# Up products of the adapters in two rounds of eight banks per group, a quarter of them added by VectorE

## The chip, the cores and the metric

The kernel runs on one core of a Trainium2 chip. The metric is the device time of one execution in microseconds. Three runs of the kernel before gave 406.56, 407.0 and 408.68 us, median 407.0 us. A separate profiled execution took 406.23 us; from its first to its last instruction it spans 404.5 us, so 1.7 us lie around the span.

## What is computed

Two layers over eight batches of 256 tokens with 1024 features, all in 32-bit floats. The first adds to `x` a linear layer whose weight carries a per-batch sign matrix. The second adds a linear layer with low-rank adapters, one pair (A, B) chosen per batch out of 32:

```python
def _L1_cond_ref(x, adapter_mapping, W, b, lora_As, lora_Bs):
    base_out = jnp.einsum('bti,oi->bto', x, W) + b
    A = lora_As[adapter_mapping]
    Bm = lora_Bs[adapter_mapping]
    lora_h = jnp.einsum('bti,bir->btr', x, A)
    lora_out = jnp.einsum('btr,bro->bto', lora_h, Bm)
    return base_out + lora_out * SCALING
x = x + _L0_cond_ref(x, L0_cond_W, L0_cond_b, condB_coeff, mask_Bx4096x4096_ik1)
x = x + _L1_cond_ref(x, itok_B_0_23, L1_cond_W, L1_cond_b, L1_cond_lora_As, L1_cond_lora_Bs)
```

The residual `x` is folded into the weights as an identity. The "down" product is `x A` (1024 to 16), the "up" product is `h B` (16 to 1024); a seventeenth row carries the bias `b`.

## The kernel before

**Layers and groups.** Two groups of four batches. In each group the first layer builds the batches' weights and multiplies (lines 269 to 532), then the second layer (`second_layer`, L702) works on the four batches at once. The second layer of the first group runs from about 114 to 208 us, that of the second from about 308 us to the end.

**The second layer.** The product of the 1024x1024 weight with 1024 features by 4 x 256 tokens is done with seven outer products instead of eight (a fast matrix multiplication), each of which is again seven inner products of 256x256 blocks with 256 tokens. `plan` (L885) lists the outer ones; I call each a pass: A11, A12, S1, S2, S4, S3, A22, numbered 0 to 6. A pass is one call of `run` (L796). It needs three accumulators in PSUM, tiles of one bank each: X (begun by `begin`, L777, at the end of the pass before), Z and Y. The seven inner products go into X, Z or Y in a fixed order; each is four matrix products, eight matmul instructions on the chip (`product`, L719). An accumulator is used again without being cleared: what is read between two products is a partial sum. So a read of X must be over before the next product into X starts.

**Reads.** `read` (L781) takes a bank to SBUF: with no other operand ScalarE copies it (L783), with one VectorE adds it (L785). Pass 0 starts sums afresh (`seed` is None: first reads are ScalarE copies); pass 4 adds onto `c12`, so all seven reads are VectorE's. VectorE also forms the sums of the right-hand blocks for later passes (`outer_sum` L889 with 128x1024 subtractions at L897; `Right.sums` L687 with four 128x512 subtractions, L693 to L699), the final additions of quarters (`add`, L882, line L883 in the profile) and, during the first group, parts of the next group's weights (`next_weights`, L907, which end in an addition at L251). These are handed to `run` as the generator `beside`, and a `next(beside, None)` stands at chosen places between the products. `ordered` (L914) puts each step behind the last VectorE read issued so far.

**PSUM.** One pool of eight banks (L85) serves all of it. A new tile takes a bank that has come free; its first matmul waits until that bank's last reader is done.

**Adapters.** In pass 0 `down` (L757) computes `h` for the four batches. `up(i, u, dest)` (L736) computes one 256-row quarter of the adapter output for all four batches: four banks G, 8 matrix products (16 matmul instructions) with 32 contraction rows each, the four batches sitting on four different groups of 32 rows. Then ScalarE copies the four banks (L755) to `c11` and `c12` (or `c21` and `c22`). It is called four times per group: in pass 0 and pass 4 as `mid` (after the product a12 into Y) and as `late` (after the product a22 into X). So a pass with adapters has the order

```
a11>X  s1>Z  s2>X  a12>Y  [round 1: 4 G]  s3>X  (a11 of next >X')  a22>X  [round 2: 4 G]  s4>Z
```

**What the copies wait for.** After pass 0, VectorE adds `e1` (the result of pass 0) to the four quarters of `c11` (L939 to L945); pass 1 accumulates on `c11`. During pass 5, `add_e5` (L973) adds `e5` (the result of pass 2) to `c22`.

**Order.** The framework schedules instructions by its own estimates. `behind(what)` (L146) nails an instruction behind an earlier one on its engine: `product(first=True)` and `up` are held behind the last inner product and the last adapter product, so TensorE's order around the adapters is fixed by the text; VectorE's order is partly free.

**Blocks of the weight.** `load_leaves` (L711) issues the seven block loads of the next pass on SyncE's queue, in the order in which the pass uses them, with the next group's mask loads between a12 and s3 (`next_masks`).

Of the kernel before, what the change touches and what calls it, by code (L numbers as in the profile page):

```python
# [14 lines left out]
P = 128  # L15
OH = 512
CG = 2
OQ = 256
# [6 lines left out]
def kernel(  # L25
# [38 lines left out]
    nc = tc.nc  # L64
    B, NG, _, _, T = xT.shape
# [5 lines left out]
    GB = 4  # L71
    NGROUP = B // GB
    S = 32
# [21 lines left out]
    h_sb = const.tile([P, T], F32, tag="h", name="h_sb")  # L95
# [22 lines left out]
    lb_pad = const.tile([P, D], F32, tag="lb", name="lb_pad")  # L118
# [20 lines left out]
    anchors = {}  # L139
# [6 lines left out]
    def behind(what: str):  # L146
        return tc.issue_after(anchors[what].ins) if what in anchors else nullcontext()
# [118 lines left out]
    def bank(name):  # L266
        return psum.tile([P, 2, T], F32, tag="ps", name=name)
# [434 lines left out]
    def second_layer(group: int, y, first, first_steps, second):  # L702
# [6 lines left out]
        left_leaf, right = {}, {}  # L709

        def load_leaves(name):  # L711
            for n in ("a11", "s1", "s2", "a12", "s3", "a22", "s4"):
                if n == "s3":
                    next_masks(max(0, plan.index(name) - 1))
                t = lpool.tile([P, CG, OQ], F32, tag="l", name=f"l{group}_{name}_{n}")
                anchors["leaves"] = nc.sync.dma_start(t, leaf_at[name, n])
                left_leaf[name, n] = t

        def product(ps, l, r, first=False):  # L719
            order = [(c, j) for c in range(CG) for j in range(2)]  # L720


            with ExitStack() as place:
                for what in ("products", "inner", "adapters") if first else ("adapters",):
                    place.enter_context(behind(what))
                for c, j in order:
                    anchors["inner"] = nc.tensor.matmul(  # L727
                        ps[:, j, :],
                        lhsT=l[:, c, j * P : (j + 1) * P],
                        rhs=r[:, c, :],  # L730
                        start=first and c == 0 and j == 0,
                        stop=False,
                        skip_group_check=True,
                    )

        def up(i, u, dest):  # L736


            ps = [bank(f"G{b}_{group}_{i}{u}") for b in range(GB)]
            with behind("inner"):  # L740
                for j in range(2):
                    o = (2 * i + u) * OQ + j * P
                    for b in range(GB):
                        rows = slice(b * S, (b + 1) * S)
                        up = nc.tensor.matmul(  # L745
                            ps[b][:, j, :],
                            lhsT=lb_pad[rows, o : o + P],
                            rhs=h_sb[rows, :],
                            start=j == 0,
                            stop=j == 1,  # L750
                            skip_group_check=True,
                        )
            anchors["adapters"] = up
            for b in range(GB):
                nc.scalar.copy(dest[b // 2][u, b % 2], ps[b])  # L755

        def down():  # L757
            ph = bank(f"psh_{group}")
# [18 lines left out]
        def begin(n, name, r):  # L777
            banks[n] = bank(f"X_{group}_{n}")
            product(banks[n], left_leaf[name, "a11"], r.b[0, 0], first=True)

        def read(out, ps, other=None):  # L781
            if other is None:
                anchors["copies"] = nc.scalar.copy(out, ps)  # L783
                return anchors["copies"]
            own["reads"] = anchors["reads"] = nc.vector.tensor_add(out, ps, other)  # L785
            return anchors["reads"]
# [6 lines left out]

        UV = [(0, 0), (0, 1), (1, 1), (1, 0)]

        def run(n, name, r, seed, out, dest=None, beside=None, early=None, mid=None, late=None, then=None):  # L796

            leaf = {k: left_leaf.pop((name, k)) for k in ("a11", "s1", "s2", "a12", "s3", "a22", "s4")}  # L800
            other = seed or {uv: None for uv in UV}
            beside = beside or iter(())
            X = banks.pop(n)

            def done(uv):
                if dest:
                    store(out[uv], *dest, *uv)
                if then:
                    then(uv)

            read(out[0, 0], X, other[0, 0])
            Z = bank(f"Z_{group}_{n}")
            product(Z, leaf["s1"], r.t["t1"], first=True)
            if early:
                early()
            product(X, leaf["s2"], r.t["t2"])
            next(beside, None)
            read(out[0, 1], X, other[0, 1])
            Y = bank(f"Y_{group}_{n}")
            product(Y, leaf["a12"], r.b[1, 0], first=True)  # L820
            read(out[0, 0], Y, out[0, 0])
            done((0, 0))
            if mid:
                mid()
            if n + 1 == len(plan):
                finish(X, Z, leaf, r, other, out, dest, beside, done)
                return
            product(X, leaf["s3"], r.t["t3"])
            next(beside, None)
            read(out[1, 1], X, other[1, 1])  # L830
            read(out[1, 1], Z, out[1, 1])
            done((1, 1))
            load_leaves(plan[n + 1])
            begin(n + 1, plan[n + 1], right[plan[n + 1]])
            next(beside, None)
            product(X, leaf["a22"], r.t["t4"])
            read(out[1, 0], X, other[1, 0])
            done((1, 0))
            next(beside, None)
            if late:  # L840
                late()
            product(Z, leaf["s4"], r.b[1, 1])
            read(out[0, 1], Z, out[0, 1])
            done((0, 1))
            for _ in beside:
                pass
# [31 lines left out]
        def quads(name):  # L878
            two = [pair(f"{name}{u}_{group}") for u in range(2)]
            return {(u, v): two[u][:, v] for u, v in UV}  # L880

        def add(o, x):  # L882
            nc.vector.tensor_add(o, o, x)  # L883

        plan = ["A11", "A12", "S1", "S2", "S4", "S3", "A22"]  # L885
        right.update({"A11": first, "A12": second, "S4": Right(f"b22_{group}", b22)})
        big_t = {}

        def outer_sum(n, x, y, name):  # L889


            big_t[n] = [
                tpool.tile([P, TPH, T], F32, tag="T", name=f"T{n}_{group}_{v}") for v in range(2)
            ]
            right[name] = Right(f"T{n}_{group}", big_t[n])
            for v in range(2):
                nc.vector.tensor_sub(big_t[n][v], x[v], y[v])  # L897
                yield
            yield from right[name].sums()
# [7 lines left out]
        def next_weights(n):  # L907
            if group + 1 < NGROUP:
                while sevens[group + 1].made < n:
                    sevens[group + 1].begin(sevens[group + 1].made + 1)  # L910
                    yield


        def ordered(steps):  # L914

            while True:
                with behind("reads" if "reads" in own else "layer"):
                    if next(steps, True):
                        return
                yield  # L920
# [10 lines left out]
        for _ in chain(islice(s3, 1), ordered(second.sums()), islice(t1, 2)):  # L931
            pass
        e1, c11, c12 = quads("e1"), quads("c11"), quads("c12")
        lower = (c11, c12)
        run(
            0, "A11", first, None, e1,
            beside=chain((None, None), islice(s3, 4)),
            early=down,
            mid=lambda: up(0, 0, lower),  # L939
            late=lambda: up(0, 1, lower),  # L940
            then=lambda uv: add(c11[0, 0], e1[0, 0]) if uv == (1, 1) else None,
        )
        for uv in UV[1:]:
            with behind("reads"):
                add(c11[uv], e1[uv])  # L945
        t2 = ordered(outer_sum(2, b22, big_t[1], "S2"))
        run(
            1, "A12", second, c11, c11,
            dest=(0, 0),
            beside=chain(t1, s3, islice(t2, 2)),  # L950
        )
        e5 = quads("e5")
        run(
# [6 lines left out]
            beside=ordered(outer_sum(3, b22, b12, "S3")),  # L960
            then=lambda uv: add(c12[uv], e1[uv]),
        )
        c21, c22 = quads("c21"), quads("c22")
        upper = (c21, c22)
        run(
            4, "S4", right["S4"], c12, c12,
            dest=(0, 1),
            beside=chain(next_weights(2), ordered(outer_sum(4, b21, big_t[2], "A22"))),
            mid=lambda: up(1, 0, upper),
            late=lambda: up(1, 1, upper),  # L970
        )

        def add_e5():  # L973

            for uv in UV:
                with behind("reads"):
                    add(c22[uv], e5[uv])
                yield

        run(5, "S3", right["S3"], e1, e1, beside=chain(add_e5(), next_weights(4)), then=lambda uv: add(c21[uv], e1[uv]))  # L980


        next_masks(6)
# [168 lines left out]
```

## Time and profile before

| what | value |
|---|---|
| median of three runs | 407.0 us (406.56 to 408.68) |
| profiled execution, its own time | 406.23 us |
| its span, first to last instruction | 404.5 us |
| TensorE busy (matmuls) | 400.5 us, 99% |
| VectorE busy | 314.4 us, 78% |
| ScalarE busy | 137.1 us, 34% |
| granted TensorE clock | 1.00 throughout |
| up products: matmul instructions, ScalarE copies | 128, 32 |
| up rounds in the first group start at | 125.06, 131.52, 175.96, 182.41 us |
| up rounds in the second group start at | 318.80, 325.26, 369.70, 376.15 us |

The span is one execution seen by the hardware profiler. "Chain" means the chain of work that ended last, followed back from the last instruction; a timeline row gives start, duration, engine, line, output and inputs, and how often. G is the tile of an up product, X, Y, Z those of the inner products, `c` and `e` the quarters of results, T and T_t the right-hand sums.

### The profile page before, as it was taken

To read this page: it belongs to the slowest core of one execution; us is meant where nothing else is said; L and a number is where in the kernel's file an instruction comes from. 1 tells how busy PE (TensorE), PEld (TensorE's weight loads), DVE (VectorE), ACT (ScalarE), POOL (GpSimd) and SP (SyncE) were. 2 spreads that over 40 slices of the span, in tenths; PEclk is the share of its full clock that TensorE was granted. 3 is DMA by queue.
4 is the path that set the end of the run, shared out by engine and by line. 5 is a ranking of instruction groups with operands and counts; after the bars stand their busy time and mean duration, and the time that the engine had idled before them with its cause. 6 is when DMAs were issued, how large, how long until landed. Compare 5 with 4: busy or idle time off the path is not lost.

```text
span 404.5 us, 6810 instructions
## 1 busy us (share of the span) xinstructions
PE 400.5 (99%) x2562; PEld 359.9 (89%) x2562; DVE 314.4 (78%) x451; ACT 137.1 (34%) x223; POOL 52.5 (13%) x103
## 2 busy tenths in 40 slices
PE   8999999999999999999999999999999999999997
PEld 6888888899978888888899999999998788888886
DVE  2447695989983789987999999999926247898595
ACT  4444525773114213132131927528221420102200
POOL 0000152105944121011040000400000000000000
PEclk9999999999999999999999999999999999999999
DMA  8999999990799799676898858632022248555754
GB/s 291 398 402 396 400 412 417 412 354 4 244 366 345 239 340 318 233 233 214 301 382 333 331 157 278 237 110 54 28 80 73 78 131 236 167 156 158 212 170 158
DMA packets 41700, 99.56 MB, mean 246 GB/s; under 512 B 5700, under 2 KB 6340, under 8 KB 41668
## 3 DMA queue, kind: packets, MB, share of 16 engines
q1 hardware_dynamic: 32978, 76.11, 55.0%
q0 software_dynamic: 6240, 18.90, 12.5%
q10 hardware_dynamic: 2450, 4.13, 2.8%
q8 instruction: 20, 0.33, 0.3%
q14 instruction: 12, 0.10, 0.1%
HBM read 79.19 MB, written 19.92 MB: 245 GB/s over the span
## 4 chain that ended last, share of the span: by engine, by line
PE 98%; DMA 1%; DVE 0%; SPq 0%; issue 0%; DVEq 0%
PE X L727 23%; PE X L427 18%; PE ps L284 14%; PE Z L727 12%; PE Z L427 9%; PE ps L309 7%; PE Y L727 6%; PE Y L427 4%; PE G L745 2%; PE psh L762 2%; PE W L868 1%; DMA w_sb<-w0T 1%; DVE w L251 0%; SPq L203 0%; DVE c L785 0%
## 5 line engine op out<-in xcount | busy, mean ns | idle before, releaser
L243 ACT ACTIVATE w<-w,neg_c,two_c 128x1024 f32<-128x1024 int32 (+2 forms) x69 | 79.1, 1183 | 60.3 <-DMA w<-mask 55.8
L251 DVE TENSOR_TENSOR w<-w,w_sb 128x1024 f32<-128x1024 f32 (+2 forms) x69 | 77.9, 1146 | 26.7 <-ACT w L243 20.7
L284 PE MATMUL ps<-x,w 128*128 128x256 f32 x256 | 55.4, 380 | 0.0
L284 PEld LDWEIGHTS ps<-x,w 128*128 128x128 f32 x256 | 48.7, 190 | 6.5
L446 ACT ACTIVATE y<-X,b_sb 128x128 f32<-128x128 f32 x60 | 17.2, 368 | 69.9 <-PE X L427 69.9
L427 PE MATMUL X<-t,s 128*128 128x128 f32 x288 | 33.9, 276 | 0.0
L883 DVE TENSOR_TENSOR c<-c,e 128x512 f32<-128x512 f32 x48 | 32.0, 685 | 1.8 <-ACT c L755 1.8
L427 PEld LDWEIGHTS X<-t,s 128*128 128x128 f32 x288 | 33.0, 192 | 0.1
L755 ACT COPY c<-G 128x512 f32<-128x512 f32 x32 | 16.4, 600 | 39.0 <-PE G L745 39.0
L309 PE MATMUL ps<-x,w 128*128 128x256 f32 x128 | 28.9, 389 | 0.1
L309 PEld LDWEIGHTS ps<-x,w 128*128 128x128 f32 x128 | 24.9, 196 | 3.9 <-DVE w L251 0.5
L783 ACT COPY e<-X 128x512 f32<-128x512 f32 x16 | 9.4, 587 | 48.6 <-PE X L727 48.6
L785 DVE TENSOR_TENSOR c<-X,c 128x512 f32<-128x512 f32 x24 | 16.3, 688 | 8.8 <-PE X L727 8.7
L727 PE MATMUL X<-T_t,l_S_s 128*128 128x256 f32 x96 | 22.7, 379 | 0.0
L427 PE MATMUL X<-t,w 128*128 128x128 f32 x192 | 22.4, 275 | 0.0
L427 PEld LDWEIGHTS X<-t,w 128*128 128x128 f32 x192 | 21.9, 192 | 0.0
L363 DVE TENSOR_TENSOR s<-w,w 128x1024 f32<-128x1024 f32 x18 | 21.7, 1222 | 0.1
L727 PEld LDWEIGHTS X<-T_t,l_S_s 128*128 128x128 f32 x96 | 18.3, 190 | 2.4
L785 DVE TENSOR_TENSOR e<-Y,e 128x512 f32<-128x512 f32 x8 | 5.5, 691 | 17.6 <-PE Y L727 17.6
L427 PE MATMUL Z<-t,s 128*128 128x128 f32 x160 | 18.9, 275 | 0.0
L427 PE MATMUL X<-x,w 128*128 128x128 f32 x160 | 18.8, 275 | 0.0
L427 PE MATMUL Y<-x,w 128*128 128x128 f32 x160 | 18.7, 276 | 0.0
(145 smaller groups left out, 673.1 us busy)
## 6 DMA issues: line engine op xcount, KB each, us to landing
w<-mask SPq DMA_DIRECT2D x60, 512.0 KB, 7.2
l_S_s<-leaf_S_s SPq DMA_DIRECT2D x32, 256.0 KB, 2.7
x<-xT SPq DMA_DIRECT2D x31, 256.0 KB, 6.6
l_A_s<-leaf_A_s SPq DMA_DIRECT2D x24, 256.0 KB, 3.1
l_S_a<-leaf_S_a SPq DMA_DIRECT2D x24, 256.0 KB, 3.2
w<-w1T SPq DMA_DIRECT2D x16, 256.0 KB, 7.2
outT<-c POOLq DMA_DIRECT2D x15, 256.0 KB, 4.8
outT<-c ACTq DMA_DIRECT2D x15, 256.0 KB, 2.3
```

Source lines behind the costliest of these rows:

```text
L243: nc.scalar.activation(w[:, i, o], m[:, i, o], AF.Identity, bias=neg_c[:, b : b + 1], scale=two_c[:, b : b + 1],)
L251: weff_at[k] = nc.vector.tensor_add(w[:, i, o], w[:, i, o], w0_of(k)[:, i, o])
L284: nc.tensor.matmul(ps[j // 2][:, j % 2, :], lhsT=w[:, c, j * P : (j + 1) * P], rhs=x_sb[b, g][:, c, :],  start=first and j % 2 == 0, stop= ...
L309: nc.tensor.matmul(ps[ot // 2][:, ot % 2, :], lhsT=w[:, h, j * P : (j + 1) * P], rhs=x_sb[0, c // CG][:, c % CG, :], start=c == 0 and ot % ...
L363: anchors["weights"] = anchors["sums"] = op(s, self.w[x, a], self.w[y, a])
L427: anchors["products"] = nc.tensor.matmul(ps[:, j, :], lhsT=w[:, c, j * P : (j + 1) * P], rhs=r, start=first and a == 0 and c == 0 and j == ...
L446: sent = nc.scalar.activation(self.out(i, v)[:, j, :], ps[:, j, :], AF.Identity, bias=b0_sb[:, ot : ot + 1])
L727: anchors["inner"] = nc.tensor.matmul(ps[:, j, :], lhsT=l[:, c, j * P : (j + 1) * P], rhs=r[:, c, :], start=first and c == 0 and j == 0, s ...
L755: nc.scalar.copy(dest[b // 2][u, b % 2], ps[b])
L783: anchors["copies"] = nc.scalar.copy(out, ps)
L785: own["reads"] = anchors["reads"] = nc.vector.tensor_add(out, ps, other)
L883: nc.vector.tensor_add(o, o, x)
```

## The change

The four rounds per group become two. Pass 0 and pass 4 get an order of their own (`late` is set): Z is read before s3, then s3 into X, s4 into Z, a22 into X, and only then, with `up(i, copied, added, to)`, both quarters (u = 0, 1) of the up product follow one another, in eight G banks. The next pass's first product `begin` comes after it. Of the eight banks, those of the two batches whose quarter belongs to the result being completed (`b // 2 == i`) are read by VectorE, which adds `e1` (pass 0) or `e5` (pass 4) in the same instruction; the other four are copied by ScalarE through `read`. The separate additions (four for `c11`, four for `c22` per group) go away. Loads of a22 and s4 change places for A11 and S4. The `beside` steps are dealt out anew: the four sums of S1 all fall into pass 0, the remaining S3 steps into pass 1, and pass 4 keeps the two 128x1024 subtractions for A22 while its four sums go to pass 5. As `up` now reads through `read`, it also moves the marks that later steps are held behind.

```diff
         def load_leaves(name):
-            for n in ("a11", "s1", "s2", "a12", "s3", "a22", "s4"):
+            order = ["a11", "s1", "s2", "a12", "s3", "a22", "s4"]
+            if name in ("A11", "S4"):
+                order[5:] = "s4", "a22"
+            for n in order:
...
-        def up(i, u, dest):
-            ps = [bank(f"G{b}_{group}_{i}{u}") for b in range(GB)]
-            with behind("inner"):
...
-            anchors["adapters"] = up
-            for b in range(GB):
-                nc.scalar.copy(dest[b // 2][u, b % 2], ps[b])
+        def up(i, copied, added, to):
+            for u in range(2):
+                ps = [bank(f"G{b}_{group}_{i}{u}") for b in range(GB)]
+                with behind("inner"), behind("adapters"):
...
+                anchors["adapters"] = last
+                for b in range(GB):
+                    uv = (u, b % 2)
+                    if b // 2 == i:
+                        read(added[uv], ps[b], to[uv])
+                    else:
+                        read(copied[uv], ps[b])
...
             read(out[0, 0], Y, out[0, 0])
             done((0, 0))
-            if mid:
-                mid()
             if n + 1 == len(plan):
                 finish(X, Z, leaf, r, other, out, dest, beside, done)
                 return
+            if late:
+                read(out[1, 1], Z, other[1, 1])
             product(X, leaf["s3"], r.t["t3"])
             next(beside, None)
-            read(out[1, 1], X, other[1, 1])
+            read(out[1, 1], X, out[1, 1] if late else other[1, 1])
+            if late:
+                done((1, 1))
+                load_leaves(plan[n + 1])
+                next(beside, None)
+                product(Z, leaf["s4"], r.b[1, 1])
+                read(out[0, 1], Z, out[0, 1])
+                done((0, 1))
+                next(beside, None)
+                product(X, leaf["a22"], r.t["t4"])
+                read(out[1, 0], X, other[1, 0])
+                done((1, 0))
+                late()
+                begin(n + 1, plan[n + 1], right[plan[n + 1]])
+                for _ in beside:
+                    pass
+                return
...
-            if late:
-                late()
...
-        lower = (c11, c12)
         run(
             0, "A11", first, None, e1,
-            beside=chain((None, None), islice(s3, 4)),
+            beside=t1,
             early=down,
-            mid=lambda: up(0, 0, lower),
-            late=lambda: up(0, 1, lower),
-            then=lambda uv: add(c11[0, 0], e1[0, 0]) if uv == (1, 1) else None,
+            late=lambda: up(0, c12, c11, e1),
         )
-        for uv in UV[1:]:
-            with behind("reads"):
-                add(c11[uv], e1[uv])
...
-            beside=chain(t1, s3, islice(t2, 2)),
+            beside=chain(s3, islice(t2, 2)),
...
+        t4 = ordered(outer_sum(4, b21, big_t[2], "A22"))
...
-            beside=chain(next_weights(2), ordered(outer_sum(4, b21, big_t[2], "A22"))),
-            mid=lambda: up(1, 0, upper),
-            late=lambda: up(1, 1, upper),
+            beside=chain(next_weights(2), islice(t4, 2)),
+            late=lambda: up(1, c21, c22, e5),
...
-        run(5, "S3", right["S3"], e1, e1, beside=chain(add_e5(), next_weights(4)), then=lambda uv: add(c21[uv], e1[uv]))
+        run(5, "S3", right["S3"], e1, e1, beside=chain(t4, next_weights(4)), then=lambda uv: add(c21[uv], e1[uv]))
```

More of the change, by code (lines that the diff above doesn't have):

```diff
@@ L734, in product @@
                     )
-        def up(i, u, dest):
-            ps = [bank(f"G{b}_{group}_{i}{u}") for b in range(GB)]
-            with behind("inner"):
-                for j in range(2):
-                    o = (2 * i + u) * OQ + j * P
-                    for b in range(GB):
[L744 to L752, printed above, removed]
-            anchors["adapters"] = up
-            for b in range(GB):
-                nc.scalar.copy(dest[b // 2][u, b % 2], ps[b])
+        def up(i, copied, added, to):
+            for u in range(2):
+                ps = [bank(f"G{b}_{group}_{i}{u}") for b in range(GB)]
+                with behind("inner"), behind("adapters"):
+                    for j in range(2):
+                        o = (2 * i + u) * OQ + j * P
+                        for b in range(GB):
+                            rows = slice(b * S, (b + 1) * S)
+                            last = nc.tensor.matmul(
+                                ps[b][:, j, :],
+                                lhsT=lb_pad[rows, o : o + P],
+                                rhs=h_sb[rows, :],
+                                start=j == 0,
+                                stop=j == 1,
+                                skip_group_check=True,
+                            )
+                anchors["adapters"] = last
+                for b in range(GB):
+                    uv = (u, b % 2)
[3 more added lines that the diff above has]
+                        read(copied[uv], ps[b])
         def down():
@@ L794, in second_layer, with run @@
         UV = [(0, 0), (0, 1), (1, 1), (1, 0)]
-        def run(n, name, r, seed, out, dest=None, beside=None, early=None, mid=None, late=None, then=None):
+        def run(n, name, r, seed, out, dest=None, beside=None, early=None, late=None, then=None):
             leaf = {k: left_leaf.pop((name, k)) for k in ("a11", "s1", "s2", "a12", "s3", "a22", "s4")}
@@ L962, in second_layer @@
         )
+        t4 = ordered(outer_sum(4, b21, big_t[2], "A22"))
         c21, c22 = quads("c21"), quads("c22")
-        upper = (c21, c22)
         run(
@@ L967, in second_layer @@
             dest=(0, 1),
-            beside=chain(next_weights(2), ordered(outer_sum(4, b21, big_t[2], "A22"))),
-            mid=lambda: up(1, 0, upper),
-            late=lambda: up(1, 1, upper),
-        )
[L973 to L978, printed above, removed]
-        run(5, "S3", right["S3"], e1, e1, beside=chain(add_e5(), next_weights(4)), then=lambda uv: add(c21[uv], e1[uv]))
+            beside=chain(next_weights(2), islice(t4, 2)),
+            late=lambda: up(1, c21, c22, e5),
+        )
+        run(5, "S3", right["S3"], e1, e1, beside=chain(t4, next_weights(4)), then=lambda uv: add(c21[uv], e1[uv]))
         next_masks(6)
```

## The prediction

> **What bounds the kernel now.** I read the page first, then the chain of waits around the up products, then the timelines of TensorE, of its weight loads, of VectorE and of ScalarE there. The page:
>
> ```profile
> PE 400.5 (99%) x2562; PEld 359.9 (89%) x2562; DVE 314.4 (78%) x451; ACT 137.1 (34%) x223; POOL 52.5 (13%) x103
> PE 98%; DMA 1%; DVE 0%; SPq 0%; issue 0%; DVEq 0%
> L883 DVE TENSOR_TENSOR c<-c,e 128x512 f32<-128x512 f32 x48 | 32.0, 685 | 1.8 <-ACT c L755 1.8
> L755 ACT COPY c<-G 128x512 f32<-128x512 f32 x32 | 16.4, 600 | 39.0 <-PE G L745 39.0
> ```
>
> TensorE is 98% of the chain. So only two things can move the time: TensorE time taken away, or a wait newly put before a matmul. The 16 µs of ScalarE copies (L755) are off the chain; halving them is worth nothing by itself. The chain in pass 0 of the first group (start, length, what):
>
> ```profile
> 123.34 1.73 PE Y L727 x8
> 125.06 1.08 PE G L745 x16
> 126.14 5.38 PE X L727 x24
> 131.52 1.08 PE G L745 x16
> 132.59 3.65 PE Z L727 x16
> ```
>
> No piece of another engine stands between. But 24 instructions of X take 5.38 here and three products of eight take 3 x 1.73 = 5.19 elsewhere; two of Z take 3.65 instead of 3.46. The timelines say where the rest is (the third row is weight loads):
>
> ```profile
> 123.17 1.89 PE L727 MATMUL Y<-y,l_A_a 128*128 128x256 f32 x8
> 124.99 1.15 PE L745 MATMUL G<-h_sb,lb_pad 32*128 32x256 f32 x16
> ...
> 124.99 0.74 PEld L745 LDWEIGHTS G<-h_sb,lb_pad 32*128 32x128 f32 x16 [0.33 <-issue]
> ...
> 126.07 2.00 PE L727 MATMUL X<-b_t,l_A_s 128*128 128x256 f32 x8
> 127.90 1.89 PE L727 MATMUL X<-y,l_A_a 128*128 128x256 f32 x8
> 129.63 0.38 PE L727 MATMUL X<-b_t,l_A_a 128*128 128x256 f32 x1
> ```
>
> From start to start an undisturbed product takes 129.63 - 127.90 = 1.73, or 0.216 a matmul. A round of 16 up matmuls is four steps of four at once: 4 x 0.216 = 0.86. From the start of Y at 123.17 to that of the second X product at 127.90 it should be 1.73 + 0.86 + 1.73 = 4.32 and is 4.73. **A round costs 0.41 µs beyond its matmuls**, for changing from 128 contraction rows to 32 and back: 0.09 before, 0.22 inside, 0.10 after. Weight loads sit idle 0.33 µs at its start, though nothing is late.
>
> **The change, step by step.** *(a) Two rounds at a time.* Matmuls stay: 128 up, the same products. Changes of form fall from eight round trips to four: 4 x 0.41 = 1.65 µs less. Bounds: 0, if the second four banks pay it again within the merged round, and 1.65; I take 1.65, since the second half has the same form as the first.
>
> *(b) Copies and additions.* ScalarE loses 16 copies of 0.60 = 9.6 µs: nothing, off the chain. VectorE loses 16 additions of 0.685 (L883) and gains 16 from banks; its additions from X (L785) have a median of 0.691, so 0.1 µs more: nothing, hidden under TensorE.
>
> [...]
>
> *(c) The order of the pass, and X's bank.* Here the cover goes. Before, after a22 only four banks were wanted, and X's was not among them: in pass 4 its read ran at 182.66 while round 2 ran from 182.34 unhindered. Now eight banks are wanted, so X's must be one. I take it to be in the second four, as it is the last to come free. The loads of a round's weights take 0.74, so the second half wants its banks 0.75 after the first load; that load comes 0.05 to 0.07 before the point where the chain lets X end, so 0.7 µs after X is ready. What the read takes is seen here for ScalarE (X ready at 131.52) and for VectorE in pass 4:
>
> ```profile
> 131.56 0.58 ACT L783 COPY e<-X 128x512 f32<-128x512 f32 x1 [2.85 <-PE X L727]
> ...
> 176.00 0.69 DVE L785 TENSOR_TENSOR c<-Y,c 128x512 f32<-128x512 f32 x1 [0.59 <-PE Y L727]
> 176.60 1.22 DVE L251 TENSOR_TENSOR w<-w,w_sb 128x1024 f32<-128x1024 f32 x1
> 179.00 0.69 DVE L785 TENSOR_TENSOR c<-X,c 128x512 f32<-128x512 f32 x1 [1.18 <-PE X L727]
> 179.72 0.69 DVE L785 TENSOR_TENSOR c<-Z,c 128x512 f32<-128x512 f32 x1
> 180.33 1.21 DVE L897 TENSOR_TENSOR T<-y,T 128x1024 f32<-128x1024 f32 x1
> 181.46 0.68 DVE L785 TENSOR_TENSOR e<-X,e 128x512 f32<-128x512 f32 x1
> 182.06 0.68 DVE L883 TENSOR_TENSOR c<-c,e 128x512 f32<-128x512 f32 x1
> 182.66 0.68 DVE L785 TENSOR_TENSOR c<-X,c 128x512 f32<-128x512 f32 x1
> 183.26 1.22 DVE L897 TENSOR_TENSOR T<-y,T 128x1024 f32<-128x1024 f32 x1
> ```
>
> Pass 0: ScalarE starts 0.04 after X, takes 0.58, and its release needs some 0.04 more (the chain's first step from VectorE to TensorE at 5.22 to 5.26): 0.66 against 0.7. No wait, in both groups.
>
> Pass 4: VectorE reads X, and it is in order. From the rows, a 128x512 step follows another after 0.60, a 128x1024 step holds the engine for 1.14. The new TensorE times follow Y's end at 175.96 in steps of 1.73: s3 at 177.69, s4 179.42, a22 181.15. First group: Y read 176.00, Z 176.60, the weight addition 177.20, X after s3 178.34 to 179.03 (a22 wants X from about 179.05, its first weights being loaded under s4's last matmul: just in time), first subtraction for A22 178.94, Z after s4 180.08, second subtraction 180.68, and only then X after a22: 181.82 to 182.51, released 182.55. The second half wants the bank at 181.85: **a wait of 0.70 µs**. Behind X's read stand VectorE's four reads of G, and for those the next pass waits; X' needs only the first G that ScalarE has copied. Second group: no weight additions, so the second subtraction falls before X after s3 and X's last read starts at once: 0.04 + 0.69 + 0.04 = 0.77 against 0.7, a wait of 0.07. Bounds for (c): 0, if VectorE is free in all four places, and 1.4 in each pass 4, if one more 128x1024 step stands in front. I take 0.77 together, from the nearest rows.
>
> *(d) Begin after the up products.* The next X' needs a bank of the first half. Those matmuls end 1.08 after X is ready; ScalarE's first copy releases it at 1.08 + 0.66 = 1.74, and X' wants it at 0.7 + 0.86 + 0.3 = 1.86. No wait; if VectorE's addition decides instead (1.08 + 0.77 = 1.85), 0.01; bound, one 128x512 step late, 0.6. In pass 0 the fourth sum of S1 takes the room of first's t4, free only after a22; VectorE does it from 0.04 to 0.73, before the first G is ready.
>
> *(e) Loads.* In pass 0 s4 is wanted at about 126.8 instead of 132.6, in pass 4 at 177.7 instead of 183.5. SyncE issues the sixth block of S4 at 167.36; landing takes 3.2 µs (5.4 for those of A11): cover of 7 µs. Nothing; it would cost its whole delay. The mask load stands ahead of it as before.
>
> *(f) Dealt-out sums.* VectorE's count per pass stays within one step: four additions go, four reads of G come; S1's sums and the S3 steps change places between passes 0 and 1. VectorE's backlog from 147 to 174 µs therefore stays what it is. Nothing; bounds ±0.3 by one half-size step.
>
> Sum: -1.65 + 0.70 + 0.07 = -0.88. Against the profiled execution's own 406.23 that is 405.35, a span of 403.6; against the median, which lies 0.77 higher, 407.0 - 0.9 = **406.1**.
>
> **Rivals.** *R1, no wait at all:* if the second subtraction is put behind X's read, only 0.07 in each pass 4 is left, -1.65 + 0.14: 405.5. For it: TensorE shows no wait for a bank now, and steps are placed where they were thought to fit. Against: that subtraction is ready 0.5 µs before X is. *R2, the saving is eaten:* VectorE's backlog delays the reads of X and of the G banks in each pass 4 by a whole 128x1024 step more, 1.14 in each, or (a) saves half: about 407.2. For it: VectorE has no idle row from 147 to 163 µs. Against: before 176 it waits for Y. *R3, slower:* one mechanism, X's bank in the first four. Then TensorE waits from the start of the round, 0.7 earlier: 0.66 in each pass 0, 0.77 and 1.4 in pass 4, together 3.5; 407.0 - 1.65 + 3.5 = 408.9. It decides against the change from 0.41 a round on. For it: the pool chooses by the scheduler's times, not the chip's. Against: today's round 2 got four other banks. *R4, no change of form is saved:* the banks of the second half come so late that the rounds fall apart; with the waits of (c) 407.8. Against: the order on TensorE is nailed.
>
> **Numbers.** Forecast (405.8 to 406.6) 0.42, R1 0.26, R2 0.14, R3 and worse 0.13, R4 0.05. Likeliest: 406.1. The range runs from R1 less 0.5 of scatter (the three runs lie 0.4 below and 1.7 above their median), 405.0, to between R4 and R3, 408.5. A change of under 0.5%, 2.0 µs, can hardly be told from none here. Faster by more needs R1 and a low draw: 0.13. Slower by more than 409.0 is R3's upper half and mishaps of order: 0.13. Within: 0.74.
>
> **What will show it.** Right: G with 32 matmuls a round, starting near 130.2, 181.1, and one 0.10 after it; no PEld wait in pass 0; in the first group's pass 4 a wait of 0.7 of G's weights on VectorE, its subtraction (L897) just ahead. Wrong: a wait in the first half (R3), a gap of 0.2 between the halves (a), a wait of X' on a reader of G (d), or of s4 on its load (e).

## The result: 0.33% slower, and the profile after

The changed kernel takes 408.14 µs (median of 22 runs) where the kernel before takes 406.59 beside it (22 runs): ratio 1.0033, 95% interval 1.0017 to 1.0048, some 1.3 µs slower by the ratio, 1.55 between the medians. The profiled execution took 408.28 µs, its span 406.6, where before it was 404.5. The forecast was 0.9 µs faster.

From the page of the changed kernel, the busy times and the chain:

```profile
PE 399.3 (98%) x2562; PEld 360.1 (89%) x2562; DVE 314.4 (77%) x451; ACT 128.6 (32%) x207; POOL 52.5 (13%) x103
PE 73%; DMA 10%; issue 7%; DVE 5%; POOL 3%; ACT 1%; SPq 0%; POOLq 0%; DVEq 0%
L791 ACT COPY c<-G 128x512 f32<-128x512 f32 x16 | 8.2, 601 | 51.7 <-PE G L749 51.7
L907 DVE TENSOR_TENSOR c<-c,e 128x512 f32<-128x512 f32 x32 | 21.9, 686 | 0.0
```

The change did what it says: 16 copies by ScalarE instead of 32, 32 separate additions by VectorE instead of 48, VectorE as busy as before to the tenth. But TensorE, 98% of the chain before, is 73% of it now. That doesn't mean that TensorE stands for a quarter of the time: it is busy for 98% of the span. The chain, followed back from a late read, leaves TensorE at 166.95 µs and runs through VectorE, a store and GpSimd into the first layer, while TensorE worked on beside it. First the rounds themselves, in the chain of the second group (start, length, what):

```profile
325.19 1.73 PE X L730 x8
326.92 1.94 PE G L749 x32
328.86 1.93 PE X L730 x8
```

From X to X that is 1.94 + 1.93, where 32 up matmuls and a product need 8 x 0.216 + 1.73 = 3.46: one excess of 0.41 for 32 matmuls instead of two. The second group's second layer runs from 311.05 to 403.75 = 92.70 µs, before from 308.12 to 401.64 = 93.52: **0.82 saved, two times 0.41, as forecast.** The loss is in the first group. TensorE's timeline there, with idle time before a row and what ended it in brackets:

```profile
154.87 1.89 PE L730 MATMUL X<-T_t,l_S_a 128*128 128x256 f32 x8
158.60 2.00 PE L730 MATMUL Z<-T,l_S_s 128*128 128x256 f32 x8 [1.84 <-DVE e L793]
160.43 1.89 PE L730 MATMUL Z<-T_t,l_S_s 128*128 128x256 f32 x8
...
163.88 1.89 PE L730 MATMUL Y<-T,l_S_a 128*128 128x256 f32 x8
166.95 1.99 PE L730 MATMUL X<-T_t,l_S_s 128*128 128x256 f32 x8 [1.17 <-DVE e L793]
```

A product starts 1.73 after the one before; here it is 3.73 and 3.07, and the product after each wait takes 0.10 more: 2.00 + 1.34 + 0.20 = 3.54 µs lost. With 1.65 saved and a second layer that began 0.20 later (114.42 against 114.22), that is +2.1, and the span grew by 2.1. Both waits are for a read by VectorE. Its timeline ahead of them:

```profile
145.32 0.68 DVE L615 TENSOR_TENSOR A<-A,A 128x512 f32<-128x512 f32 x1
146.44 0.69 DVE L793 TENSOR_TENSOR c<-Z,c 128x512 f32<-128x512 f32 x1 [0.44 <-PE Z L730]
147.04 2.35 DVE L921 TENSOR_TENSOR T<-y,T 128x1024 f32<-128x1024 f32 x2
152.92 0.69 DVE L604 TENSOR_TENSOR A<-A 128x512 f32<-128x512 f32 x1 [3.52 <-DMA leaf_S_a<-A]
153.53 0.69 DVE L693 TENSOR_TENSOR T_t<-T,T 128x512 f32<-128x512 f32 x1
154.13 1.41 DVE L604 TENSOR_TENSOR A<-A,A 128x512 f32<-128x512 f32 x2
155.46 0.68 DVE L793 TENSOR_TENSOR e<-Y,e 128x512 f32<-128x512 f32 x1
...
157.86 0.69 DVE L793 TENSOR_TENSOR e<-Z,e 128x512 f32<-128x512 f32 x1
```

The S3 steps are of two kinds. Four form the blocks of S3 (L615); three of these are stored as they are by GpSimd (`leaf_S_a<-A`, L541). Four more overwrite the blocks "in place" with sums and differences of them (L604). VectorE stands 3.52 µs, from 149.4 to 152.92, in front of the first step in place, which overwrites a block that is still being stored. From then on it works without a gap; the read of Z that TensorE wants comes at 157.86, and Z's next product starts at 158.60. The chain names the store:

```profile
145.70 0.54 POOL outT L800
...
146.29 6.53 DMA leaf_S_a<-A
...
152.92 0.69 DVE A L604
```

GpSimd issues this store at 146.29, because VectorE formed the block only from 145.32 to 146.00 (L615); it lands 6.5 µs later. Both count: had it landed in the 3.7 µs that such stores took before (median), VectorE would have stood some 0.7, an estimate (3.52 less 6.5 - 3.7). In the trace of before, two rows tell the other side:

```profile
136.74 0.54 POOL L541 DMA_DIRECT2D leaf_S_a<-A  x1 [4.10 <-DVE A L615]
...
147.25 0.68 DVE L604 TENSOR_TENSOR A<-A 128x512 f32<-128x512 f32 x1
```

The last of the three stores was issued at 136.74, ten microseconds ahead of the step that overwrites. The change took the S3 steps out of pass 0, where two of the four blocks had been formed by 131.8, and gave that room to the sums of S1.

### The profile page after: what moved, and what is told of

Read it like the earlier page. It is cut to its first block, busy times and chain, and to the rows that moved or that the text cites. A ratio compares the mean times of both kernels' runs of the same rounds, so it can differ in the third digit from the quotient of the medians.

```text
span 406.6 us, 6798 instructions
## 1 busy us (share of the span) xinstructions
PE 399.3 (98%) x2562; PEld 360.1 (89%) x2562; DVE 314.4 (77%) x451; ACT 128.6 (32%) x207; POOL 52.5 (13%) x103
## 4 chain that ended last, share of the span: by engine, by line
PE 73%; DMA 10%; issue 7%; DVE 5%; POOL 3%; ACT 1%; SPq 0%; POOLq 0%; DVEq 0%
PE X L730 17%; PE X L427 14%; PE Z L730 9%; PE ps L284 8%; PE Z L427 7%; PE ps L309 6%; PE Y L730 4%; PE Y L427 4%; DMA w<-mask 3%; DMA x<-xT 2%; DMA leaf_A_s<-A_s 2%; DMA leaf_S_a<-A 2%; PE G L749 1%; DMA leaf_S_s<-w 1%; POOL leaf_S_a L541 1%
## 5 line engine op out<-in xcount | busy, mean ns | idle before, releaser
L791 ACT COPY e<-X 128x512 f32<-128x512 f32 x14 | 8.2, 586 | 56.6 <-PE X L730 56.6
L791 ACT COPY c<-G 128x512 f32<-128x512 f32 x16 | 8.2, 601 | 51.7 <-PE G L749 51.7
L907 DVE TENSOR_TENSOR c<-c,e 128x512 f32<-128x512 f32 x32 | 21.9, 686 | 0.0
```

## The experiments

*Theories.* The store theory: the new deal of the steps makes VectorE, in order, stand for a store. The bank theory: eight banks at once and VectorE's reads of them cost the time. The backlog theory: passes 1 and 2 simply hold too many VectorE steps, and the store is by the way. Each ratio below is to the kernel before, run beside it on the same chip.

**e1, the deal undone.** The changed kernel with the old deal beside passes 0 and 1.

```diff
-            beside=t1,
+            beside=chain((None, None), islice(s3, 4)),
...
-            beside=chain(s3, islice(t2, 2)),
+            beside=chain(t1, s3, islice(t2, 2)),
```

> The changed kernel with the steps beside passes 0 and 1 dealt as in the kernel before (four S3 steps beside pass 0; the four sums of S1, then the other S3 steps beside pass 1). Store theory (VectorE stands for the landing of a stored S3 block because the S3 steps came later): the two waits of TensorE in the first group (2.0 and 1.34 us) go, 1.65 us of changes of form stay saved, 0.2 of restarts go too: 1.5 us faster than the kernel before, ratio 0.996. Bank theory (eight banks and their reads by VectorE cost the time): no change against the changed kernel, ratio 1.003.

Measured: 406.13 against 406.75, ratio 0.9985 (0.9975 to 0.9995). The two waits are gone, which the bank theory did not allow, but only 0.6 of 1.5 µs was won. The forecast was 0.996. In the trace VectorE stands again, elsewhere, for a load:

```profile
130.89 0.69 DVE L615 TENSOR_TENSOR A<-A,A 128x512 f32<-128x512 f32 x1 [2.84 <-DMA A<-w1T]
131.50 0.68 DVE L793 TENSOR_TENSOR e<-Z,e 128x512 f32<-128x512 f32 x1
```

The S3 step waits for a loaded block of the weight, and behind it stands the read of Z. Here the mechanism of step (c) shows, on another bank than (c) had: Z's bank is wanted by the second half of the round. The weight loads of that round, and of the product after it:

```profile
130.65 1.16 PEld L749 LDWEIGHTS G<-h_sb,lb_pad 32*128 32x128 f32 x20 [0.33 <-issue]
132.24 0.73 PEld L749 LDWEIGHTS G<-h_sb,lb_pad 32*128 32x128 f32 x12 [0.42 <-DVE e L793]
133.44 1.59 PEld L730 LDWEIGHTS X<-y,l_A_a 128*128 128x128 f32 x8 [0.47 <-DVE c L793]
```

The round and the product behind it wait for a VectorE read each: from the start of G at 130.65 to that of X at 133.44 it takes 2.79, in the changed kernel 1.94 (130.38 to 132.32). These 0.85 µs are nearly all that is missing of the 1.5. So the old deal does not fit the new order of the pass either: in the old order these S3 steps had no round of eight behind them.

**e2, the deal alone.** The kernel before, its four rounds and its copies kept, with only the S3 steps and the sums of S1 dealt as in the changed kernel.

```diff
-            beside=chain((None, None), islice(s3, 4)),
+            beside=t1,
...
-            beside=chain(t1, s3, islice(t2, 2)),
+            beside=chain(s3, islice(t2, 2)),
```

> The kernel before, four rounds and copies as they were, with only the S3 steps of pass 0 moved to pass 1 and the sums of S1 to pass 0, as in the changed kernel. Store theory: VectorE stands for 3 to 4 us on a stored S3 block near 150 us and TensorE waits some 3.4 us in passes 2 and 3: 3 to 3.5 us slower than before, ratio 1.008. Bank theory: no difference, ratio 1.000.

Measured: 409.55 against 406.75, ratio 1.0066 (1.0051 to 1.0081): 2.7 µs slower, without one round merged; the store theory had said 3 to 3.5. The same wait and the same two stops:

```profile
153.02 0.69 DVE L604 TENSOR_TENSOR A<-A 128x512 f32<-128x512 f32 x1 [3.40 <-DMA leaf_S_a<-A]
...
158.70 1.99 PE L727 MATMUL Z<-T,l_S_s 128*128 128x256 f32 x8 [1.71 <-DVE e L785]
...
167.05 1.99 PE L727 MATMUL X<-T_t,l_S_s 128*128 128x256 f32 x8 [1.17 <-DVE e L785]
```

These two waits with their slower restarts make 3.4 µs in the trace (1.87 + 1.33 + 0.20), and so much longer is its span (407.9 against 404.5). The changed kernel has to lose some 3.0 to be 1.3 slower with 1.65 saved; 2.7 of it (all of it, within the intervals) comes from two lines of the change that have nothing to do with rounds or banks. The bank theory falls.

**e3 and e7, the stored block formed first.** The changed kernel, the same steps beside the same passes; of the four S3 blocks the one that is overwritten first is formed first. TensorE, ScalarE and SyncE keep their order; on GpSimd the last of the three stores comes 3 µs earlier than in the changed kernel (143.25 for 146.29).

```diff
-            yield from outer("S3", nc.vector.tensor_sub, a11, a21, a21)
+            yield from outer("S3", nc.vector.tensor_sub, a11, a21, {uv: a21[uv] for uv in ((1, 1), (0, 0), (0, 1), (1, 0))})
```

> The changed kernel, the same steps beside the same passes, but the S3 block that is stored and then overwritten first is formed first of the four, so that its store is issued some 10 us earlier. Order on TensorE, ScalarE and SyncE is the same. Store theory: VectorE's wait of 3.5 us falls to under 0.5, ratio 0.996 to 0.997. Backlog theory (too many VectorE steps in passes 1 and 2, the wait for the store is by the way): VectorE does as many steps in the same passes, at most 1 us is won, ratio 1.001 to 1.003.

Measured: 405.68 against 406.75, ratio 0.998 (0.9964 to 0.9995). That is nearer to the store theory's 0.996 to 0.997 than to the 1.001 to 1.003 of the backlog theory, and reaches the former only with its interval. In the trace TensorE has no wait in the second layers and the span is 402.7, 1.8 under that of before; but this profiled execution, 404.41, is the fastest of the twelve, which go up to 407.76. The block that is overwritten first is now stored first, at 135.61, and VectorE goes on without standing:

```profile
135.61 0.54 POOL L541 DMA_DIRECT2D leaf_S_a<-A  x1 [9.86 <-DVE A L615]
...
145.00 0.68 DVE L615 TENSOR_TENSOR A<-A,A 128x512 f32<-128x512 f32 x1
...
146.72 0.68 DVE L604 TENSOR_TENSOR A<-A 128x512 f32<-128x512 f32 x1
147.32 1.22 DVE L921 TENSOR_TENSOR T<-y,T 128x1024 f32<-128x1024 f32 x1
```

The same number of steps in the same passes, and no wait: the store theory holds for the wait. The kernel ran again, beside e5 and e6:

> The kernel of e3 once more, beside e5 and e6 on one chip, as the version that should beat both kernels: 1.65 us of changes of form saved and no wait put in, ratio 0.996 (405.1 where before takes 406.75); by its first measurement 0.998.

Measured: 405.05 against 406.61, ratio 0.9963 (0.9947 to 0.9978). Its times lie between 404.31 and 406.55, and the profiled execution, 406.29, shows what the slower ones can have. Its chain:

```profile
146.59 7.91 DMA l_S_a<-leaf_S_a
...
154.64 3.69 PE X L730 x16
```

A block of 0.26 MB takes 7.9 µs to land, and its product starts at 154.64, 1.3 late. From 145 to 155 µs the DMA engines are full in this kernel (1.03 and 1.04 of their time, 401 and 408 GB/s), in before 0.99 and 0.98 at 348 and 324 GB/s. The full stretch alone does not make the wait: the fast execution of e3 has 1.02 and 1.05 there, at 400 and 402 GB/s, and TensorE waits for nothing. Why some executions have a late block and others not stays open.

**e4, the steps in place later.** The changed kernel, with these four steps moved to pass 2.

```diff
-            beside=chain(s3, islice(t2, 2)),
+            beside=chain(islice(s3, 4), islice(t2, 2)),
...
-            beside=chain(t2, ordered(right["S4"].sums())),
+            beside=chain(t2, s3, ordered(right["S4"].sums())),
```

> The changed kernel with the four S3 steps in place moved from pass 1 to pass 2, behind the sums of S2. Store theory: the store has landed before the first step in place comes up, no wait: ratio 0.996 to 0.997. Backlog theory: four more steps in pass 2, in which VectorE has no idle time: TensorE waits at least as long as in the changed kernel, ratio 1.003 or more.

Measured: 407.45 against 406.75, ratio 1.0013 (1.0004 to 1.0023). VectorE no longer stands for a store, yet TensorE still waits, once:

```profile
162.50 1.89 PE L730 MATMUL Y<-T,l_S_a 128*128 128x256 f32 x8
166.18 1.99 PE L730 MATMUL X<-T_t,l_S_s 128*128 128x256 f32 x8 [1.79 <-DVE e L793]
```

Neither expectation was met: the store theory had 0.996 to 0.997, the backlog theory 1.003 or more. The wait for the store is not all, and the backlog theory has its part. In this trace VectorE has no gap from 154.7 to 169 µs; the four steps, 4 x 0.60 = 2.4 µs, come at 160.0 to 163.6 in the midst of it, and the product into X at 166.18 is late by 1.95, nearly as much. The 3.5 µs for the store hurt for the same reason: in the changed kernel too VectorE has no gap behind them in which to make them up.

**e5, the rounds split again.** e3's kernel with a round of four before a22 and one of four after it.

```diff
+                late((0,))
                 product(X, leaf["a22"], r.t["t4"])
                 read(out[1, 0], X, other[1, 0])
                 done((1, 0))
-                late()
+                late((1,))
```

> The kernel of e3 (no wait left on TensorE in its trace) with each round of eight banks split again into two of four: the first half between s4 and a22, the second after a22. If a round costs 0.41 us beyond its matmuls, four more rounds cost 1.65 us: ratio to before 1.000 to 1.002, and 0.004 above the kernel of e3 in the same call. If e3's gain comes from elsewhere (reads, order of the pass), it stays within 0.5 us of the kernel of e3.

Measured: 406.81 against 406.61, ratio 1.0021 (1.0002 to 1.004), 1.76 µs above e7, run beside it, between the medians, and 2.4 by the ratios; the two intervals allow 1.0 to 3.8, and four of e5's twelve runs lie at 408.4 or above. TensorE waits for no bank. Its chain in pass 0:

```profile
129.36 1.08 PE G L749 x16
130.44 1.92 PE X L730 x8
132.36 1.08 PE G L749 x16
133.44 1.92 PE X L730 x8
```

Every round has its 0.41 again (1.08 + 1.92 less 0.86 + 1.73). Merging is worth what was forecast: shown by the rows, and within what the times allow.

**e6, copies instead of additions from banks.** e3's kernel, with all eight banks copied by ScalarE and `e1` or `e5` added from SBUF, right behind the reads of the round.

```diff
-                        read(added[uv], ps[b], to[uv])
+                        read(added[uv], ps[b])
...
+                for uv in ((u, 0), (u, 1)):
+                    with behind("reads"):
+                        add(added[uv], to[uv])
```

> The kernel of e3, with all eight banks of a round copied by ScalarE and e1 or e5 added by VectorE from SBUF in separate instructions, as before the change. If the additions from banks are worth nothing by themselves (ScalarE off the chain, VectorE's count the same): within 0.3 us of the kernel of e3, ratio 0.996 to 0.998. If they carry the gain: slower by 0.5 us or more, with TensorE waiting for a bank that ScalarE reads.

Measured: 408.29 against 406.61, ratio 1.0038 (1.0025 to 1.0051): 3.2 µs slower than e7. Step (b) had priced this at nothing. VectorE and TensorE around pass 4 of the first group:

```profile
185.09 1.29 DVE L910 TENSOR_TENSOR c<-c,e 128x512 f32<-128x512 f32 x2 [1.94 <-ACT c L794]
187.05 1.29 DVE L910 TENSOR_TENSOR c<-c,e 128x512 f32<-128x512 f32 x2 [0.67 <-ACT c L794]
188.26 0.68 DVE L796 TENSOR_TENSOR e<-X,e 128x512 f32<-128x512 f32 x1
...
189.00 1.99 PE L730 MATMUL X<-T_t,l_S_s 128*128 128x256 f32 x8 [1.01 <-DVE e L796]
```

Eight copies one after another take ScalarE 4.01 µs (the 32 matmuls fill the banks in 1.94). VectorE, in order, stands for them with its additions, and the read of the next pass's X stands behind: 1.2 late, and so in both groups. With the slower restarts that is 1.27 and 1.32 µs, and 0.29 more behind each round of pass 0, together 3.2. TensorE, however, waits for VectorE, not for a bank of ScalarE's, which was the sign that I had named. And e6 is not the kernel before in this point: there the additions of `e5` were dealt out beside pass 5, here they stand right behind the round. So e6 shows what eight copies cost with the additions directly behind them; whether additions dealt out later would cost anything, no run shows.

**e8, the stores earlier still.** e3's kernel, with two S3 blocks right behind pass 0's round, two at the start of pass 1, the steps in place last.

```diff
-            beside=t1,
+            beside=chain(t1, islice(s3, 2)),
...
-            beside=chain(s3, islice(t2, 2)),
+            beside=chain(islice(s3, 2), islice(t2, 2), s3),
```

> The kernel of e3 with the four S3 blocks formed and stored earlier still: two right behind the reads of pass 0's round, two at the start of pass 1, before the two subtractions for S2; the four steps in place come last in pass 1. In e7's profiled execution a load of 0.26 MB landed only after 7.9 us, with DMA full from 145 to 155 us, and TensorE waited 1.45 us. If the stores crowd that stretch, moving them 3 to 5 us ahead takes the late landings away: ratio 0.995 to 0.996 and all times within 1 us. If the scatter has another cause: as e3 and e7, 0.996 to 0.998, with times up to 2 us above the fastest.

Measured: 405.45 against 406.76, ratio 0.9968 (0.9956 to 0.998), times 404.91 to 406.63. No better than e3 and e7 by more than the intervals allow, and with a spread of 1.7 µs: nearer to the second expectation, another cause, but six runs don't decide it. In its profiled execution, 406.63, the DMA engines are less full from 145 to 155 µs (0.97 and 0.93, 371 and 335 GB/s), and no block is late there. But it has the next wait of the kind: VectorE stands 1.16 µs for a loaded weight block that landed 7.3 µs after its issue, and TensorE 1.1 behind it, at 137.67. So the kernels of e3 and e8 are the versions that beat both kernels, the one before by 0.2 to 0.4%.

## Why the prediction was wrong, point by point

- *(a) Two rounds at a time, -1.65.* Right: 0.82 in the second group of the trace, and every one of e5's split rounds pays its 0.41 again (1.76 between the medians of e7 and e5). The halves of a round have no gap between them (1.94 for 32).
- *(b) Copies and additions, nothing.* As a count right: VectorE's busy time is unchanged, and in the changed kernel an addition from G takes as long as any other (median 682 ns, the separate additions 686). As a value it is open: I priced the copies against the old order, where ScalarE had time between two rounds of four (in pass 0 of the first group four copies take 2.05 µs from 126.16, and the next four start at 132.61). With rounds of eight, copies alone and additions right behind them cost 3.2 µs (e6), twice what merging saves; (b) holds for the changed kernel, but not for every way of reading eight banks.
- *(c) X's bank, +0.77.* Wrong in size, it was 0: no round of the changed kernel waits for X's bank, and those of pass 4 take 1.94 in both groups (from 184.48 and 377.40). My timetable for VectorE in pass 4 put Z's read after Y's and came out 0.6 late; it was done in the idle time before Y. From Y's read to X's last I had 5.82 (176.00 to 181.82); it was 5.20 in the changed kernel (179.34 to 184.54) and 5.21 in e3. The mechanism itself is there (e1, 0.42 on Z's bank). So R1's "no wait" came about, though not by the order that R1 named: the second subtraction still stands ahead of X's read.
- *(d), (e) Begin and loads, nothing.* Right in the changed kernel. The load that is 1.3 late in e7 is one of pass 3's, which (e) did not look at.
- *(f) Dealt-out sums, "nothing; bounds ±0.3 by one half-size step".* **This is the step that failed**, and none of the rivals held it: put at nothing, it cost 3.54 µs in the trace, 2.7 by itself (e2). With it the sum comes out: -1.65 + 0 for (c) + 3.54 + 0.20 for the later start = +2.1, as the span grew. I counted VectorE's steps per pass, and the count was right. I did not ask what else each moved step issues and waits for: an S3 step ends in a store by GpSimd's queue, and the step in place waits for that store to land. Both rows stood in the trace of before, the store at 136.74 and the step at 147.25, ten microseconds apart. Moving the former by a pass ate the ten. (f) saw that VectorE has no room from 147 to 174 µs, but not that a wait put ahead of that stretch reaches TensorE whole.
- The range (405.0 to 408.5) held 408.14 by luck: R3, the slower rival, put the loss in TensorE's waits for X's bank, which did not occur. R2's "about 407.2" is no sum of its terms either: 1.14 in each pass 4 gives 408.4, half of (a) 406.9. The direction was wrong.

## What to carry to other kernels

When a change deals small steps out anew, write beside each moved step the transfer it starts and the later step that waits for this transfer, and compare their distance with the landing time in the fullest stretch (here 6.5 µs instead of 3.7). Ask also whether the engine that stands has idle time behind the wait: here VectorE had none in which to make it up, and handed the whole of it on. It stood 3.52 µs and TensorE lost 3.54. And count a saving on the bounding engine only together with the reads it calls for: in e6 eight banks read by one engine, with additions right behind, cost 3.2 µs, twice the 1.65 that the merging saved.

## What the runs showed of the hardware that I had not expected

- A block of 0.26 MB landed in 6.5 µs (the store in the changed kernel) and 7.9 µs (a load in e7) in the stretch from 145 to 155 µs, where the DMA engines moved 402 and 385 GB/s in the changed kernel, 401 and 408 in e7; between 100 and 190 µs of before the median was 3.2 to 3.5 for loads of the blocks of S1 to S4, and 3.7 for the same stores. In e3, at 400 and 402 GB/s in that stretch, TensorE waited for no load.
- A round of 32 up matmuls costs no more for its changes of form than one of 16: 0.41 µs, once (1.94 + 1.93 less 3.46 in the changed kernel, 1.08 + 1.92 less 0.86 + 1.73 in e5).
